# A two-layer scan kernel: sums over states taken once per turn, by halves, in shared PSUM banks

## The chip, the cores and the metric

The kernel runs on one core of a Trainium2 chip. The metric is the time of one execution on the device in microseconds (us). Engines are named as the profile does: PE (matrix), DVE (vector), ACT (activation), POOL (GpSimd), SP (issues the DMAs).

## The reference

A network of four layers works on images of shape (4, 96, 64, 64). Layer 0 is a convolution and selective scan with 192 channels and 16 states; layers 2 and 3 are spectral, attention and feed-forward blocks on tokens. The change concerns layer 1 alone, which applies this block (`ss2d`) twice in a row:

```
xz = x @ in_w.T;  xa, z = split(xz)
xc = silu(dwconv3x3(xa))                      # 96 channels, 4096 tokens
xs = 4 directions of xc: rows, columns, and both reversed
dts, Bs, Cs = split(xproj_w @ xs)             # 6, 8 and 8 rows
delta = softplus(dt_w @ dts + dt_b)
h[l] = exp(delta * A) * h[l-1] + delta * B[l] * xs[l]      # 8 states per channel
y[l] = sum over states of h[l] * C[l]  + D * xs[l]
out = (layernorm(sum of y over the 4 directions) * silu(z)) @ out_w.T
```

## The kernel before

Three stages follow each other: `stage_mamba` (layer 0), `stage_ss2d` (layer 1), `stage_tokens` (layers 2 and 3). The first two share the class `Scan`.

In layer 1 there are 8 blocks (4 images, 2 applications), 4 directions each, and 4 stretches of T = 1024 tokens per direction: 128 *turns*. A turn has 96 channels with 8 states, that is 768 rows, worked off as 6 *units* of 128 rows (16 channels by 8 states). So layer 1 has 768 units. For each unit:

- `load`: a DMA brings delta, each row spread over 8 partitions, into `sc_d` (6 buffers); for the third and the sixth unit of a turn another brings the inputs into `sc_u` (2 buffers).
- `decay`: ACT takes the exponential, in place in `sc_d`, or into PSUM for the third and sixth unit.
- `inputs`: for the other four units PE spreads the input over states, two matmuls of 512 columns into a tile `s` of two PSUM banks. There are 2 buffers of `s`; the third and sixth unit use one for the decay. `s` is free again once the unit's scan is done.
- `scan`: DVE multiplies `s` by B (rows in `bc`), then runs the scan over 1024 tokens, in place in `sc_d` (or `sc_u`). For the third and the sixth unit POOL does the multiplication by B in `sc_u`.
- `outputs`: POOL multiplies the states by C (the other half of `bc`) into a product `sc_h` (5 buffers, 4 KB per partition each).
- `reduce`: after every three units (a *round*) PE sums the products over states with a 0/1 table `c_red`: three matmuls side by side, into 32 rows each, for both halves of 512 tokens. The sums of both rounds accumulate in the tile `y`, [128, 1024] in two PSUM banks, one buffer.
- `end`: DVE adds `y` to `ysum`, 96x1024 at once; in the two directions by columns the access to `ysum` is strided.

In the profile a float32 matmul appears as two MATMUL rows. PSUM's eight banks before: two buffers of `s` (4 banks), one of `y` (2), two of `mm` (1 each). `mm` is shared by all other matmuls of layer 1: the projection to delta, B and C (`delta<-mm`), the row of C spread over partitions (`mm<-bc_stack,selbc`, copied to `bc` by ACT), a temporary of the splitting into bfloat16 parts (`bc_in`, `bc_part`), and the work between the scans of two blocks (convolution `mm<-xp,w_conv`, gates `ysum<-mm`, layer norm, output projection).

Nearly all instructions of layers 0 and 1 carry line 466, as they are recorded first (`Plan`) and issued by a helper. Their order on each engine is made beforehand: `Plan.order` simulates the five engines with a cost per operation and lets every engine take the ready operation with the lowest index, the index being the place in the program. A tile of `mm` is a *hold*: the simulation gives it one of the ring's buffers when the first operation is taken and frees it after the last; the first one waits for everything that later operations of the hold with lower-indexed inputs need. Buffers of other tags (`sc_h`, `s`, `y`, `bc_stack`) go round in fixed order. On the chip each engine then runs its list strictly in that order. DMAs are all issued from SP's queue.

The program order is given by `Scan.run`, step by step. In step s: loads of unit s+5; the paced work of the turn or block; `reduce` of the round that ends with unit s−3; `end` of the turn that ends with unit s−4; `scan` of unit s; decay and inputs of unit s+2; `outputs` of unit s.

The row of C of a turn passes through `narrow` (split into three bfloat16 parts, written to DRAM, read back as `bc_stack`, 2 buffers) and `mix` (two matmuls into `mm`, two copies to `bc`).

Of the kernel before, what the change touches and what calls it, by code (L numbers as in the profile page):

```python
# [11 lines left out]
F32 = mybir.dt.float32  # L12
BF16 = mybir.dt.bfloat16
# [4 lines left out]
PSUM = bass.MemoryType.PSUM  # L18
DRAM = bass.MemoryType.DRAM

NB, C, HW, L = 4, 96, 64, 4096
T, W = 1024, 512
NT, NW = L // T, L // W
DIN, NS0, RK = 192, 16, 6
NS1, NDIR = 8, 4
# [157 lines left out]
class Work:  # L183


    def __init__(self, steps, count, due):
        self.steps, self.count, self.due = steps, count, due
        self.taken, self.since, self.done = 0, None, False
# [92 lines left out]
class Plan:  # L281
# [174 lines left out]
    def run(self, tc):  # L456
        def placed(v, holds):
            hold = holds.get(v.tensor.name) if isinstance(v, bass.AP) else None
            return bass.AP(hold.buffer.tensor, v.offset, v.ap) if hold else v

        with tc.manual_schedule():
            for op in self.order():
                for method, a, kw in op.calls:
                    a = [placed(v, op.holds) for v in a]
                    kw = {n: placed(v, op.holds) for n, v in kw.items()}
                    getattr(getattr(self.nc, op.engine), method)(*a, **kw)  # L466
# [88 lines left out]
def split_steps(nc, x, parts, ps):  # L555


    p, n = x.shape
    for part in parts[0:2]:
        nc.scalar.copy(part, x)  # L560
        yield
        off = ps.tile([p, n], F32, tag="mm", name="off_ps")
        nc.scalar.copy(off, part)
        nc.vector.tensor_tensor(x, x, off, ALU.subtract)
        yield
    nc.scalar.copy(parts[2], x)
    yield
# [26 lines left out]
class Scan:  # L594
# [6 lines left out]

    LOOK = 5

    def __init__(self, k, rep, ps, n_state, red, bufs):
        self.k = k
        self.rep, self.ps, self.red, self.bufs = rep, ps, red, bufs
        self.ns, self.dl = n_state, 128 // n_state
        self.per = 32 // self.dl
        self.yps = None
# [37 lines left out]

    def decay(self, u):
        if not u.spread:
            u.s = self.ps.tile([128, T], F32, tag="s", name="s_ps", bufs=2)  # L650
            self.nc.scalar.activation(u.s, u.d, AF.Exp, scale=u.turn.acol(u.j))
        else:
            self.nc.scalar.activation(u.d, u.d, AF.Exp, scale=u.turn.acol(u.j))

    def inputs(self, u):
        u.s = self.ps.tile([128, T], F32, tag="s", name="s_ps", bufs=2)
        with self.nc.side_by_side(overlap=self.halves(u)):
            for h, (table, du) in enumerate(u.turn.spread(u)):
                self.nc.tensor.matmul(u.s[:, h * W:(h + 1) * W], table, du, start=True, stop=True)
# [24 lines left out]
    def reduce(self, us):  # L684
# [8 lines left out]
        for hs in halves:  # L693
            with nc.side_by_side():
                for h in hs:
                    for u in us:
# [3 lines left out]
                            start=not held, stop=r == self.per - 1, skip_group_check=True,  # L700
                        )

    def run(self, units, plan):


        nc = self.nc
        works = []
        for s in range(-self.LOOK, len(units) + 5):
            def at(n):
                return units[n] if 0 <= n < len(units) else None  # L710

            works += plan(s)
            u = at(s + self.LOOK)
            if u:
                if u.first:
                    u.turn.ready.finish()
                self.load(u)
            for w in works:
                w.pace(s)
            works = [w for w in works if not w.done]  # L720
            u = at(s - 3)
            if u and u is u.round[-1]:
                self.reduce(u.round)
            u = at(s - 4)
            if u and u.last:
                u.turn.end(u.q, self.yps)
            u = at(s + 2)
            if u and u.spread:
                self.decay(u)
            u = at(s)  # L730
            if u:
                self.scan(u)
            u = at(s + 2)
            if u:
                if not u.spread:
                    self.decay(u)
                else:
                    self.inputs(u)
            if u and not u.spread:
                nc.gpsimd.tensor_tensor(u.u, u.u, u.turn.bc[:, 0, :], ALU.mult)  # L740
            u = at(s)
            if u:
                self.outputs(u)
        for w in works:
            w.finish()
# [292 lines left out]
def stage_ss2d(ctx: ExitStack, k: Common, x: bass.AP, mid: bass.AP, bn: bass.AP, mid2: bass.AP):  # L1038
# [3 lines left out]
    nc, tc = k.nc, k.tc  # L1042
    wp = ctx.enter_context(tc.tile_pool(name="s_w", bufs=1))
    big = ctx.enter_context(tc.tile_pool(name="s_big", bufs=1))
    pl = Plan(nc)
    big = pl.pool(big, 2)
    wk = pl.pool(ctx.enter_context(tc.tile_pool(name="s_wk", bufs=1)), 2)
    rep = pl.pool(ctx.enter_context(tc.tile_pool(name="s_rep", bufs=1)), 4)
    dr = pl.pool(ctx.enter_context(tc.tile_pool(name="s_dr", bufs=1, space=DRAM)), 3)
    ps = pl.pool(ctx.enter_context(tc.tile_pool(name="s_ps", bufs=1, space=PSUM)), 2, {"mm": [128, W]})  # L1050
    NCH = C // 16
    PW = HW + 2

# [3 lines left out]
    out_w = k.load(wp, "w_out1")  # L1057
    group = k.load(wp, "c_group")
    sel = k.load(wp, "c_sel1")
    sc = Scan(k, rep, ps, NS1, k.load(wp, "c_red1"), (6, 2, 5))  # L1060
    nc.scalar.activation(acol, acol, AF.Exp)
    nc.vector.tensor_scalar(acol, acol, -1.0, None, ALU.mult)
    selbc = wp.tile([3 * NS1, 128], BF16, name="selbc")
# [33 lines left out]
    nc = k.nc = pl  # L1097
# [4 lines left out]
    class Block:  # L1102


        def __init__(self, b, i):
            self.b, self.i, self.rows = b, i, 0
            self.ready = None
# [111 lines left out]
    class Tokens(Turn):  # L1219
# [56 lines left out]
        def narrow(self):  # L1276

            x = wk.tile([64, 128], F32, tag="bc_in", name="bc_in", bufs=1)
            part = [(128, 8), (T, NS1), (1, 128)]
            at = self.dd[C + NS1:CD, :]  # L1280
            nc.sync.dma_start(out=x, in_=bass.AP(at.tensor, at.offset, part))
            yield
            parts = [wk.tile([64, 128], BF16, tag="bc_part%d" % n, name="bc_part", bufs=1) for n in range(3)]
            yield from split_steps(nc, x, parts, ps)
            sd = dr.tile([3, NS1, T], BF16, tag="bcd", name="bcd", bufs=3)
            for n, p in enumerate(parts):
                nc.sync.dma_start(out=bass.AP(sd.tensor, sd[n].offset, part), in_=p)
            self.stack = wk.tile([3 * NS1, T], BF16, tag="bc_stack", name="bc_stack", bufs=2)
            nc.sync.dma_start(out=self.stack, in_=sd.rearrange("n r t -> (n r) t"))

        def mix(self):
# [10 lines left out]
                nc.scalar.copy(self.bc[:, 1, at:at + W], pb)  # L1302
                yield

        def end(self, q, yps):
            ysum, t, yps = self.block.ysum, self.t, yps[0:C, :]
            cs = slice(t * T, (t + 1) * T)
            if self.d == 0:
                nc.vector.scalar_tensor_tensor(
                    ysum[:, cs], self.block.xc[:, cs], dsum[:, self.block.i:self.block.i + 1], yps,  # L1310
                    ALU.mult, ALU.add,
                )
            elif self.d % 2 == 0:
                nc.vector.tensor_tensor(ysum[:, cs], ysum[:, cs], yps, ALU.add)
            else:
                n_w = T // HW
                view = ysum.rearrange("p (h w) -> p w h", w=HW)[:, n_w * t:n_w * (t + 1), :]
                nc.vector.tensor_tensor(view, view, yps.rearrange("p (w h) -> p w h", h=HW), ALU.add)

    blocks = [Block(b, i) for pair in ((0, 1), (2, 3)) for i in range(2) for b in pair]  # L1320
# [6 lines left out]
    units = [u for turn in turns for u in sc.units(turn, (groups,))]  # L1327
# [326 lines left out]
@with_exitstack  # L1654
def kernel(ctx: ExitStack, tc: tile.TileContext, x: bass.AP, w: dict, out: bass.AP):
    k = Common(ctx, tc, w)
    dp = ctx.enter_context(tc.tile_pool(name="mids", bufs=1, space=DRAM))
    mid = dp.tile([NB, C, L], F32, name="mid")
    mid2 = dp.tile([NB, C, L], F32, name="mid2")
    bn = k.cp.tile([C, 2], F32, name="bn_scale")  # L1660
    stage_mamba(k, x, mid, bn)
    stage_ss2d(k, x, mid, bn, mid2)
    stage_tokens(k, mid2, out)
# [22 lines left out]
```

## Time and profile before

| | |
|---|---|
| median of three runs | 7542.12 us (7540.26 to 7549.51) |
| profiled execution | 7571.38 us, span 7569.0 us |
| layer 0, layer 1, layers 2 and 3 in the span | 0 to 2890, 2890 to 6235, 6235 to 7569 us |
| busy over the span | PE 6648.2, DVE 5764.4, POOL 5765.3, ACT 4499.9 us |
| mean granted PE clock | 0.905 |

The profile is one execution. In its page the span is cut into 40 slices, with a digit for the busy tenths of each engine. A group row has the operation, out<-in by tile names, shapes, count, busy us and mean ns, then the engine's idle time before it and who ended it. A wait row has who waited for whom, the total in us, the times and the longest. A timeline row has start, duration, engine and operation, and in brackets the idle time before it and its releaser. A window row has the stretch, its length, the busy us of PE, PE's weight loads, DVE, ACT and POOL, the granted clock, the busy share of the DMA engines and GB/s.

### The profile page before, as it was taken

The numbers are of one execution on the slowest core, as the hardware profiler recorded it, in microseconds if no ns is written. First come the engines' busy times: TensorE is split into PE (matmuls) and PEld (weight loads), VectorE is DVE, ScalarE is ACT, GpSimd is POOL, SyncE is SP. The second block draws the span as 40 slices with busy tenths as digits, with TensorE's granted clock in tenths as the row PEclk, the third lists the DMA queues.
The fourth block names the chain that finished last, engine by engine and source line by source line (L and its number), as shares of the span: only waits on it lengthen the run. The fifth ranks groups of instructions, "written<-read, shape, count | busy, mean of one in ns | idle before, by whom it ended". The sixth has DMA issues, their size and how long they took to land. (4 is left out here: it accounts for less than half of the span.)

```text
span 7569.0 us, 84054 instructions
## 1 busy us (share of the span) xinstructions
PE 6648.2 (88%) x28616; PEld 2867.8 (38%) x28616; DVE 5764.4 (76%) x4491; ACT 4499.9 (59%) x6656; POOL 5765.3 (76%) x2836
## 2 busy tenths in 40 slices
PE   8888888988888877989898898989898868999997
PEld 3322233323323222323232333323232228778784
DVE  6989988988898985898887878788888863344342
ACT  4655555555555544777777676677777644445442
POOL 6989988989998985889897978889898870232323
PEclk9999999999999998999898898989898888889897
DMA  7988988988888886999898989899999960000000
GB/s 192 239 224 232 230 216 220 239 222 226 227 235 217 222 224 168 233 241 230 223 234 222 244 218 241 215 230 232 230 238 238 236 176 22 1 18 5 15 9 9
DMA packets 448078, 1418.13 MB, mean 187 GB/s; under 512 B 81626, under 2 KB 91539, under 8 KB 445600
## 3 DMA queue, kind: packets, MB, share of 16 engines
q1 hardware_dynamic: 447648, 1412.76, 72.7%
q8 instruction: 225, 3.69, 0.2%
q14 instruction: 205, 1.68, 0.1%
HBM read 1238.48 MB, written 174.06 MB: 187 GB/s over the span
## 5 line engine op out<-in xcount | busy, mean ns | idle before, releaser
L466 POOL TENSOR_TENSOR sc_h<-sc_d,bc 128x1024 f32<-128x1024 f32 x1024 | 2406.9, 2360 | 394.8 <-DVE sc_d L466 186.0
L466 DVE TENSOR_TENSOR_SCAN sc_d<-sc_d,carry,s 128x1024 f32<-128x1024 f32 x768 | 1799.7, 2344 | 74.7 <-ACT sc_d L466 18.2
L466 DVE TENSOR_TENSOR s<-s,bc 128x1024 f32<-128x1024 f32 x1024 | 1248.7, 1220 | 505.3 <-PE s L466 500.2
L466 PE MATMUL s<-du,c_sel 96*128 96x512 f32 x2048 | 1124.0, 678 | 226.6 <-DVE sc_d L466 127.3
L466 ACT ACTIVATE sc_d<-sc_d,w_alog 128x1024 f32<-128x1024 f32 x1024 | 1165.7, 1144 | 257.4 <-DMA sc_d<-dd 253.7
L466 POOL TENSOR_TENSOR sc_h<-sc_u,bc 128x1024 f32<-128x1024 f32 x512 | 1208.0, 2359 | 112.2 <-PE y L466 73.1
L466 POOL TENSOR_TENSOR sc_u<-sc_u,bc 128x1024 f32<-128x1024 f32 x512 | 1208.2, 2360 | 100.9 <-DMA sc_u<-ud 87.6
L466 PE MATMUL y<-sc_h,c_red 128*32 128x512 f32 x6144 | 1094.5, 656 | 87.2 <-POOL sc_h L466 83.2
L466 DVE TENSOR_TENSOR_SCAN sc_u<-s,carry,sc_u 128x1024 f32<-128x1024 f32 x384 | 895.2, 2331 | 36.7 <-ACT s L466 17.5
L466 PE MATMUL s<-du,c_selp 128*128 128x512 f32 x1408 | 729.8, 647 | 112.3 <-DVE sc_d L466 108.8
L466 PEld LDWEIGHTS s<-du,c_sel 96*128 96x128 f32 x2048 | 396.2, 208 | 869.8 <-issue 427.7
L466 ACT ACTIVATE s<-sc_d,w_alog 128x1024 f32<-128x1024 f32 x512 | 570.8, 1115 | 240.7 <-DVE sc_d L466 155.7
L466 ACT ACT_TABLE_LOAD x499 | 640.2, 1283 | 8.7
L466 DVE TENSOR_TENSOR_SCAN sc_d<-sc_d,s 128x1024 f32<-128x1024 f32 x256 | 583.1, 2282 | 23.0 <-ACT sc_d L466 6.2
L508 POOL TENSOR_TENSOR ln_rs<-ln_rs_e,mhalf 128x4 f32<-128x4 f32 x128 | 134.9, 1056 | 582.9 <-DVE ln_rs_e L506 581.2
L466 PE MATMUL mm<-xp,w_conv 96*96 96x512 f32 x1152 | 528.7, 600 | 4.6 <-ACT bc L466 2.2
L466 PEld LDWEIGHTS y<-sc_h,c_red 128*32 128x32 f32 x6144 | 197.7, 114 | 848.9 <-issue 529.7
L466 ACT COPY carry<-sc_d 128x1 f32<-128x1 f32 x768 | 142.8, 186 | 565.5 <-DVE sc_d L466 564.0
L466 PEld LDWEIGHTS s<-du,c_selp 128*128 128x128 f32 x1408 | 263.2, 201 | 539.4 <-issue 274.7
L466 PE MATMUL mm<-hn,conv_w 97*64 97x512 f32 (+1 forms) x1024 | 368.8, 615 | 22.5 <-DVE hn L466 22.5
L466 PEld LDWEIGHTS mm<-xp,w_conv 96*96 96x96 f32 x1152 | 185.3, 164 | 310.1 <-issue 295.5
L466 DVE TENSOR_TENSOR_SCAN sc_u<-s,sc_u 128x1024 f32<-128x1024 f32 x128 | 290.7, 2271 | 14.1 <-ACT s L466 7.9
(211 smaller groups left out, 9343.6 us busy)
## 6 DMA issues: line engine op xcount, KB each, us to landing
sc_d<-dd SPq DMA_DIRECT2D x1536, 512.0 KB
sc_u<-ud SPq DMA_DIRECT2D x512, 512.0 KB
bc<-dd SPq DMA_DIRECT2D x128, 512.0 KB
dd<-delta SPq DMA_DIRECT2D x128, 448.0 KB
bc<-bcd SPq DMA_DIRECT2D x64, 512.0 KB
ud<-du SPq DMA_DIRECT2D x192, 128.0 KB
dd<-delta SPq DMA_DIRECT2D x32, 512.0 KB
ud<-du SPq DMA_DIRECT2D x32, 512.0 KB
```

The source lines that it names most:

```text
L466: getattr(getattr(self.nc, op.engine), method)(*a, **kw)
L508: nc.gpsimd.tensor_tensor(rs, ve, self.mhalf[:p, 0:n], ALU.pow)
```

## The change

In layer 1 the sums are no longer taken round by round. All six products of a turn are kept, and in the step of unit s = last + 2 a new method `sums` takes them all: for each half of 512 tokens it opens a tile of `mm` (one bank), accumulates the two rounds in it, and calls `end` for that half, which adds 96x512 to `ysum`. The tile `y` is not used in layer 1 any more; its two banks go to `mm`, which has 4 buffers. `sc_h` gets 8 buffers instead of 5, `bc_stack` 1 instead of 2. `s` keeps its 2 buffers. Layer 0 uses the same class with the old behaviour.

```diff
-    def __init__(self, k, rep, ps, n_state, red, bufs):
+    def __init__(self, k, rep, ps, n_state, red, bufs, spreads=2, late=False):
...
+    def sums(self, us):
+
+        nc = self.nc
+        for h in range(T // W):
+            yps = self.ps.tile([128, W], F32, tag="mm", name="y_ps")
+            for r in range(self.per):
+                with nc.side_by_side():
+                    for u in us:
+                        if u.r == r:
+                            row, _, at = u.rows[h]
+                            nc.tensor.matmul(
+                                yps[row:row + 32, :], self.red[:, r, :], u.c[:, at:at + W],
+                                start=r == 0, stop=r == self.per - 1, skip_group_check=True,
+                            )
+            us[0].turn.end(h, yps)
...
+            u = at(s - 2)
+            if self.late and u and u.last:
+                self.sums(units[s - 1 - len(u.round) * self.per:s - 1])
             u = at(s - 3)
-            if u and u is u.round[-1]:
+            if not self.late and u and u is u.round[-1]:
                 self.reduce(u.round)
             u = at(s - 4)
-            if u and u.last:
+            if not self.late and u and u.last:
                 u.turn.end(u.q, self.yps)
...
-    ps = pl.pool(ctx.enter_context(tc.tile_pool(name="s_ps", bufs=1, space=PSUM)), 2, {"mm": [128, W]})
+    ps = pl.pool(ctx.enter_context(tc.tile_pool(name="s_ps", bufs=1, space=PSUM)), 4, {"mm": [128, W]})
...
-    sc = Scan(k, rep, ps, NS1, k.load(wp, "c_red1"), (6, 2, 5))
+    sc = Scan(k, rep, ps, NS1, k.load(wp, "c_red1"), (6, 2, 8), 2, True)
...
-            self.stack = wk.tile([3 * NS1, T], BF16, tag="bc_stack", name="bc_stack", bufs=2)
+            self.stack = wk.tile([3 * NS1, T], BF16, tag="bc_stack", name="bc_stack", bufs=1)
...
-        def end(self, q, yps):
-            ysum, t, yps = self.block.ysum, self.t, yps[0:C, :]
-            cs = slice(t * T, (t + 1) * T)
+        def end(self, h, yps):
+            ysum, yps, at = self.block.ysum, yps[0:C, :], self.t * T + h * W
+            cs = slice(at, at + W)
...
-                n_w = T // HW
-                view = ysum.rearrange("p (h w) -> p w h", w=HW)[:, n_w * t:n_w * (t + 1), :]
+                view = ysum.rearrange("p (h w) -> p w h", w=HW)[:, at // HW:(at + W) // HW, :]
```

More of the change, by code (lines that the diff above doesn't have):

```diff
@@ L602 @@
     LOOK = 5
-    def __init__(self, k, rep, ps, n_state, red, bufs):
-        self.k = k
+    def __init__(self, k, rep, ps, n_state, red, bufs, spreads=2, late=False):
+        self.k, self.spreads, self.late = k, spreads, late
         self.rep, self.ps, self.red, self.bufs = rep, ps, red, bufs
@@ L649, in decay @@
         if not u.spread:
-            u.s = self.ps.tile([128, T], F32, tag="s", name="s_ps", bufs=2)
+            u.s = self.ps.tile([128, T], F32, tag="s", name="s_ps", bufs=self.spreads)
             self.nc.scalar.activation(u.s, u.d, AF.Exp, scale=u.turn.acol(u.j))
@@ L655, in inputs @@
     def inputs(self, u):
-        u.s = self.ps.tile([128, T], F32, tag="s", name="s_ps", bufs=2)
+        u.s = self.ps.tile([128, T], F32, tag="s", name="s_ps", bufs=self.spreads)
         with self.nc.side_by_side(overlap=self.halves(u)):
```

## The prediction

> **What bounds the kernel now.** I read the page's slices first, then the busy time by stretch, then the waits inside the stretch that the change touches, then the groups there, and last one turn in the timeline.
>
> ```profile
> span 7569.0 us, 84054 instructions
> ...
> PE   8888888988888877989898898989898868999997
> ...
> DVE  6989988988898985898887878788888863344342
> ...
> POOL 6989988989998985889897978889898870232323
> PEclk9999999999999998999898898989898888889897
> ```
>
> PE, DVE and POOL are all busy for eight to nine tenths until slice 32, and no slice shows one of them alone at its limit. The change touches only layer 1. Its scan runs from about 2890 us to 6235 us.
>
> ```profile
> core 0: us, PE busy (x) PEld busy (x) DVE busy (x) ACT busy (x) POOL busy (x), PEclk, DMA share, GB/s
> 0.00:2890.00 2890.00, 2520.65 (x8660) 853.49 (x8660) 2534.01 (x1606) 1597.27 (x2170) 2546.34 (x1124) 0.93 0.86 222
> 3020.00:6180.00 3160.00, 2758.23 (x8098) 943.33 (x8097) 2681.46 (x1815) 2226.11 (x3326) 2794.27 (x1271) 0.91 0.91 230
> 5400.00:5800.00 400.00, 363.86 (x1086) 124.37 (x1087) 349.29 (x235) 290.81 (x439) 369.58 (x168) 0.92 0.94 237
> ```
>
> The second row is the full-speed part of layer 1: 128 turns in 3160 us, 24.7 us each. Per turn PE is busy 21.5 us, DVE 20.9, POOL 21.8; each idles 3 to 4 us. The three hand work to each other through small buffers, so a time lost on one is partly lost on all. The third row is the fastest stretch: DMA moves 237 GB/s where the mean is 230.
>
> ```profile
> DVE s L466 <- PE s L466: 266.4, 165, 5.0
> ...
> PE s L466 <- DVE sc_d L466: 127.3, 75, 7.2
> ...
> POOL sc_h L466 <- ACT bc L466: 90.1, 26, 9.5
> ...
> POOL sc_h L466 <- PE y L466: 82.2, 32, 6.6
> ...
> PE mm L466 <- ACT bc L466: 28.8, 39, 4.0
> ```
>
> These are waits in 3020:6180 (total us, times, longest). The largest is DVE's on `s`: two buffers of `s` go round between PE and DVE. PE can refill one only after a scan frees it, and DVE needs it one unit later. The `mm` waits are PE waiting for a shared bank to be emptied.
>
> ```profile
> 4998.59 3.78 PE L466 MATMUL s<-du,c_sel 96*128 96x512 f32 x4 [2.87 <-DVE sc_d L466]
> ...
> 5002.30 1.03 PE L466 MATMUL mm<-bc_stack,selbc 24*128 24x512 bf16 x2
> ...
> 5004.09 4.66 POOL L466 TENSOR_TENSOR sc_h<-sc_d,bc 128x1024 f32<-128x1024 f32 x2 [9.46 <-ACT bc L466]
> ```
>
> Here POOL stands 9.46 us for a row of C (`bc`) whose matmul ran late among the shared banks. PE, after 2.87 us of idleness, took 3.78 us for a fill of `s` that takes 1.98 us elsewhere (at 4319.04).
>
> **The change, part by part.** I weigh each effect over 128 turns. Because three engines take turns at being the bound, a removed wait on one counts by about 0.4 (my choice, between a third and a half).
>
> *Matmuls of the sums.* They are 24 per turn before and after (3,072 in all), in groups of three side by side. PE work: 0. What changes is when they run. Before, a round of three products is summed by 12 matmuls in about 2.3 us (rows of 1.92, 2.29 and 2.69 us in the timeline), twice per turn at different steps. After, all 24 become ready at once with the turn's sixth product, about 4.6 us, and they come in program order ahead of the fill of `s` of the same step. A fill takes 2.2 us (1112.5 us for 506). DVE covers it with a multiply and a scan, 1.22 + 2.34 = 3.56 us. Before, a fill that meets a round is late by at most 2.3 + 2.2 − 3.56 = 0.94 us, twice a turn; after, by at most 4.6 + 2.2 − 3.56 = 3.24 us, once. Taking half of each as the mean: 0.94 against 1.62 us per turn, so **+86 us**. Bounds: 0, if all falls into PE's 3.1 us of idleness per turn, and 3.24 × 128 = +415 us, if each meets in full.
>
> *PE's wait.* All sums now wait for one product. Behind them on PE stand the next fills and DVE waits for those. The present wait of matmul `y` on POOL is 25.6 us in 27 times; I leave it, between 0 and twice that.
>
> *The clock.* The half of the turn that loses a round has more idleness: 1.6 + 2.3 = 3.9 us, in pieces. The row at 4998.59 shows that 2.87 us of idleness went with a fill 1.8 us longer. The Trainium skill ("TensorE: Matmul & The Clock Gate", section on HAM oscillation) allows gaps up to about 3.4 us. By the rule these pieces cost 0. By the row, if one turn in five gets such a gap, 26 × 1.8 = 46 us of PE time, 0.4 of it on the path. I follow the row: **+20 us**, bounds −58 (clock from 0.91 to 0.95, half on the path) to +58.
>
> *Evacuations on DVE.* One 96x1024 read becomes two of 96x512. Contiguous: 2 × 0.67 (`ysum<-ysum,mm` has 669 ns) for 1.24 us; strided: 2 × 1.27 (`t<-t,o`, 1269 ns) for 2.40 us. That is 0.10 × 64 + 0.14 × 64 = 15 us, and 8 us on the path. Behind each on DVE stand multiply and scan; the second eviction can wait for the second half of the sums. The present wait is 33.1 us in 24 times; up to once more of it, taken at +7. Together **+15 us**.
>
> *Products kept.* POOL makes the same six per turn (2.36 us each). Before, five buffers: the third and the sixth product of a turn wait for a round's release. After, eight buffers: only the third product of the next turn waits, again with two products in between, but for the third of four groups instead of the second of two, 1.15 us later. From 82.2 us in 32 times (2.6 us each) I make 16 times 3.75 = 60 us: −22 × 0.4 = **−9 us**, bounds −82 and +150.
>
> *Four shared banks.* This is the gain. PE waits for banks: 28.8 (`bc`) + 17.7 (`ysum`) + 16.4 (`delta`) + 14.0 (`bc_in`) + 10.2 (DVE `ysum`) = 87.1 us; POOL's wait on `bc` is 90.1 us. Together 177.2 us, the most these rows can give back; the least is 0, as the sums now take two of the banks for a few us per turn and some of these waits are for data. The same page of the skill, same section, reports that doubling PSUM buffers gave no further gain in its kernel. By the rule 0, by the rows 0.4 × 177 = 70. I take the rows, for they name the bank's reader: **−70 us**.
>
> *One `bc_stack` instead of two.* Its load on SP's queue now also waits for the last `bc` matmul of the turn before; queued behind it are `sc_d` and `sc_u` loads. In the late turn shown, the stack was issued at 4988.14 and read at 5002.30; the next is due a turn (24.7 us) after, so some 10 us of margin remain even there. Cost 0; without that margin POOL's waits on `sc_u` (31.9 us) could double: +30. No DMA is added or moved otherwise.
>
> Sum: 86 + 20 + 15 − 9 − 70 = **+42 us**. The profiled execution took 7571.4 us (span 7569.0 and 2.4 around), 29 us over the median of 7542.1; against itself the sum gives 7613, against the median 7584.
>
> **The rivals.**
>
> *B, the banks win.* The order of instructions is made by a list scheduler; with four banks it can fill PE's gaps (402 us idle in 3160) with shared matmuls, so fewer fills are late. For it: two of three engines' waits name banks; the latest `bc` turns idle POOL for 9 us. Against it: the largest wait, 266 us on `s`, keeps its two buffers. Price: 0.6 × 177 = −106, the burst at a third, +30: 7466 us. It cannot go far: the fastest stretch moves 237 against 230 GB/s, 3% of 3160, or some 95 us.
>
> *C, the products come free too late.* One mechanism: POOL makes two products and one or two multiplies after the last product, 7.1 to 9.4 us, and then needs the third group of sums done. In the turn shown the last product of a round ended at 4992.3 and its round at 4995.7, 3.4 us; one more group makes 4.6, inside 7.1. It decides from the point where PE's queue delays the sums by over 2.5 us. At 1.2 us per turn POOL gives away 154 us: 7696 us. For it: the 6.6 us maximum of that wait; against: the wait has half as many places.
>
> *D, no change.* The scheduler spreads the groups between fills, and bank relief and delays cancel: 7542 us.
>
> **How the numbers follow.** A (the sum, 7584; its own range 7558 to 7650) has 0.40; B 0.36; C 0.15; D 0.09. A and B differ in two sizes only, the burst's and the banks'; I put A ahead because the burst is bounded by 0 and +415, far wider above my value than below, while the banks cannot give more than 177. About 0.2% (15 us) is what a measurement can tell: faster 0.36, same 0.10 (D and the edge of A), slower 0.54. The range reaches from 7430 (B with nearly all of the relief) to 7725 (C with A's evictions).
>
> **What would show it.** Right: in layer 1 DVE's wait on `s` rises from 266 us by 50 to 150; POOL's wait on `bc` falls below 60; PE's waits on ACT for `mm` fall below half; the sums appear as runs of about 24 matmuls; `ysum` evictions at 0.67 and 1.27 us; PEclk at or below 0.91. Wrong: DVE's wait on `s` falls and the 3160 us stretch shortens (B), or POOL's wait on the sums passes 150 us (C). 0 to 2890 us must stay as it is; if it moves, the whole reading is off.

## The result: no change, and the profile after

The changed kernel takes 7540.5 us (median of 12 runs), the kernel before 7546.8 us (12 runs). The ratio is 0.9993, with a 95% interval from 0.9982 to 1.0004: no difference that can be measured. I had forecast 7584 us, +0.5%; the time lies inside the range, but no rise came. What came true is rival D, to which I had given 0.09. Below, each ratio is to the kernel before, run beside the kernel in question, and ratios are turned into microseconds on 7546.8 us.

The page of the profile after, the same rows as were shown of before:

```profile
span 7542.1 us, 84090 instructions
...
PE   8888889988888887989797798989898769999997
...
DVE  6989988988898985888888888888898863344342
...
POOL 6989988989898985889897879889898960232323
PEclk9999999999999998989898898989897878889897
```

No digit differs from before by more than one. The stretches and the waits of layer 1 tell more. First the stretches (length, busy us of PE, weight loads, DVE, ACT, POOL, then granted clock, DMA share, GB/s):

```profile
0.00:2890.00 2890.00, 2512.39 (x8660) 852.60 (x8660) 2537.01 (x1617) 1597.61 (x2171) 2548.31 (x1126) 0.94 0.85 222
...
3020.00:6180.00 3160.00, 2729.15 (x8153) 980.89 (x8151) 2684.59 (x1942) 2230.46 (x3339) 2792.34 (x1273) 0.88 0.91 230
```

Layer 0 is as it was. In layer 1 the engines do in 3160 us almost exactly what they did before (POOL 2792.3 against 2794.3 us, DVE 2684.6 against 2681.5), but PE runs at a granted clock of 0.88 instead of 0.91. The waits of the changed kernel in 3020:6180 (total us, times, longest):

```profile
DVE s L466 <- PE s L466: 261.6, 178, 4.2
PE s L466 <- DVE sc_d L466: 260.3, 101, 7.1
...
DVE ysum L466 <- PE mm L466: 77.8, 65, 4.5
POOL sc_h L466 <- ACT bc L466: 68.7, 21, 8.8
...
POOL sc_h L466 <- PE mm L466: 40.4, 25, 3.4
...
PE mm L466 <- DMA bc_stack<-bcd: 30.8, 18, 6.6
...
PE mm L466 <- ACT bc L466: 6.8, 9, 1.7
```

The four banks did what they were to do. The five waits of PE on a bank's reader that made 87.1 us before are now 6.8 (`bc`) + 3.3 (`ysum`) + 1.2 (`delta`) + 4.4 (`bc_in`) + 2.6 (DVE `ysum`) = 18.3 us; POOL's wait on `bc` fell from 90.1 to 68.7 us and its wait on the sums from 82.2 to 40.4 us. But PE's wait for a scan to free a buffer of `s` doubled, from 127.3 to 260.3 us. What the banks gave, PE stands about again, elsewhere. Its idle time in the stretch is about what it was (402 us before, 431 after), but in the timeline the pieces longer than 2 us have grown from 48 (150 us together) to 78 (291 us).

The timeline also shows the late sums themselves (start, duration, then engine, operation and count of rows; the fills are two together):

```profile
3170.48 3.63 PE L466 MATMUL mm<-sc_h,c_red 128*32 128x512 f32 x24
3174.05 3.81 PE L466 MATMUL s<-du,c_sel 96*128 96x512 f32 x8
```

In about half of the turns all 24 rows of a turn's sums stand in one run like this; in most of the others they come as two runs of 12, with other matmuls between.

So the change has either two effects of opposite sign, or only effects that nothing depends on. The experiments were made to tell these apart.

### The profile page after: what moved, and what is told of

It is laid out like the page before. It is cut to its first block, busy times and chain, and to the rows that moved or that the text cites. A ratio compares the mean times of both kernels' runs of the same rounds, so it can differ in the third digit from the quotient of the medians.

```text
span 7542.1 us, 84090 instructions
## 1 busy us (share of the span) xinstructions
PE 6589.2 (87%) x28616; PEld 2890.5 (38%) x28616; DVE 5771.9 (77%) x4619; ACT 4498.6 (60%) x6664; POOL 5765.3 (76%) x2836
## 5 line engine op out<-in xcount | busy, mean ns | idle before, releaser
L466 PE MATMUL s<-du,c_sel 96*128 96x512 f32 x2048 | 1180.1, 711 | 313.9 <-DVE sc_d L466 260.3
L466 PEld LDWEIGHTS s<-du,c_sel 96*128 96x128 f32 x2048 | 420.7, 220 | 985.3 <-issue 434.5
L466 DVE TENSOR_TENSOR_SCAN sc_d<-sc_d,s 128x1024 f32<-128x1024 f32 x256 | 582.9, 2282 | 29.5 <-ACT sc_d L466 13.4
L466 PE MATMUL mm<-sc_h,c_red 128*32 128x512 f32 x3072 | 533.4, 638 | 14.7 <-POOL sc_h L466 11.6
L466 PE MATMUL y<-sc_h,c_red 128*32 128x512 f32 x3072 | 489.5, 658 | 58.0 <-POOL sc_h L466 57.6
L466 POOL TENSOR_TENSOR du<-delta,xc 96x1024 f32<-96x1024 f32 (+2 forms) x128 | 266.8, 2089 | 91.4 <-ACT delta L466 48.7
L466 DVE TENSOR_TENSOR ysum<-ysum,mm 96x512 f32<-96x512 f32 x256 | 248.1, 972 | 80.2 <-PE mm L466 78.9
```

## The experiments

**First batch: the two halves of the change.** Theory T1: the four banks gain, the late sums lose, and the two cancel. Theory T2: the exchange of `s` holds layer 1, and it is indifferent to both.

*e1_late_mm2*, the change with two shared banks:

```diff
-    ps = pl.pool(... name="s_ps" ..., 4, {"mm": [128, W]})
+    ps = pl.pool(... name="s_ps" ..., 2, {"mm": [128, W]})
```

> The change with two shared banks instead of four, so only the sums at the turn's end, the eight products and the halves are left. Theory T1 (the four banks gain and the late sums lose, and the two cancel): slower than before by 50 to 120 us, as the loss stands alone, with PE's waits on shared banks above the 87 us of before. Theory T2 (layer 1 is held by the exchange of the two buffers of s between PE and DVE, to which both parts are indifferent): within 20 us of before, with DVE's wait on s at 250 to 280 us in 3020:6180.

Measured: 7790.8 us, ratio 1.0331 (1.0309 to 1.0352), +250 us. T2 is out: the late sums without the two banks lose more than twice what T1 said at most. The waits of this kernel show the loss in all three engines, DVE on `s`, POOL on the sums, PE on banks:

```profile
DVE s L466 <- PE s L466: 341.9, 191, 7.0
...
POOL sc_h L466 <- PE mm L466: 105.6, 41, 7.3
...
PE mm L466 <- ACT bc L466: 36.8, 49, 2.5
```

*e2_late_s3*, the freed banks given to a third `s` instead:

```diff
-    ps = pl.pool(... name="s_ps" ..., 4, {"mm": [128, W]})
+    ps = pl.pool(... name="s_ps" ..., 2, {"mm": [128, W]})
-    sc = Scan(k, rep, ps, NS1, k.load(wp, "c_red1"), (6, 2, 8), 2, True)
+    sc = Scan(k, rep, ps, NS1, k.load(wp, "c_red1"), (6, 2, 8), 3, True)
```

> The change with the two banks that were freed given to a third buffer of s, and two shared banks. T2: DVE's wait on s (262 us after the change) falls below 130 us, and the time falls by 60 to 150 us. T1: a third s does little (within 30 us of the kernel with two shared banks and two s), as the banks and the burst decide.

Measured: 7652.8 us, ratio 1.0142 (1.0120 to 1.0164). Against e1 a third `s` is worth 143 us, so `s` does matter, as T2 said; but the same two banks used as shared ones are worth 255 us. DVE's wait on `s` fell from 341.9 to 191.3 us, not below 130.

*e3_sums_behind_fill*, the sums moved in the step:

```diff
-            u = at(s - 2)
-            if self.late and u and u.last:
-                self.sums(...)
             u = at(s - 3)
...
             if u and not u.spread:
                 nc.gpsimd.tensor_tensor(u.u, u.u, u.turn.bc[:, 0, :], ALU.mult)
+            u = at(s - 2)
+            if self.late and u and u.last:
+                self.sums(...)
```

> The change, with the sums placed behind the fill of s of the same step in program order instead of ahead of it. T1 (the burst ahead of the fill costs): faster than the change by 30 to 90 us, DVE's wait on s below 200 us. T2: within 20 us of the change.

Measured: 7535.3 us, ratio 0.9992 (0.9981 to 1.0003), the same as the change. That the sums stand ahead of the fill in program order costs nothing that can be measured. My picture of the burst, a block of sums in front of a fill of the same step, is not shown to be how the late sums lose.

*e4_before_keep8*, the kernel before with the buffers of the change:

```diff
-    sc = Scan(k, rep, ps, NS1, k.load(wp, "c_red1"), (6, 2, 5))
+    sc = Scan(k, rep, ps, NS1, k.load(wp, "c_red1"), (6, 2, 8))
-            self.stack = wk.tile(... name="bc_stack", bufs=2)
+            self.stack = wk.tile(... name="bc_stack", bufs=1)
```

> The kernel before with eight buffers of sc_h instead of five and one of bc_stack instead of two, nothing else. Both theories: POOL's wait on the sums (82 us in 3020:6180) goes to near zero. T1: worth 0.4 of it, 20 to 40 us. T2: within 15 us of before.

Measured: 7524.3 us, ratio 0.9975 (0.9959 to 0.9990), −19 us. POOL's wait on `y`, 82.2 us before, is no longer among its waits; so a wait of 82 us, wholly removed, was worth some 19 us. One `bc_stack` costs nothing that shows here.

**Second batch: sharing, or lateness?** Theory S: e1 loses because the sums sit in the banks that the others need. Theory L: because the sums are late and in one piece.

*e5_late_own2_mm2* and *e6_late_own1_mm3*, the late sums in banks of their own:

```diff
-            yps = self.ps.tile([128, W], F32, tag="mm", name="y_ps")
+            yps = self.ps.tile([128, W], F32, tag="y", name="y_ps", bufs=2)   # e6: bufs=1
-    ps = pl.pool(... name="s_ps" ..., 4, {"mm": [128, W]})
+    ps = pl.pool(... name="s_ps" ..., 2, {"mm": [128, W]})                    # e6: 3
```

> The late sums by halves in two banks of their own and two shared banks for the rest: the PSUM of before, with only the moment of the sums, the halves and the products changed. Theory S (the 251 us lost with two shared banks come from the sums sitting in the banks that the other matmuls need): within 25 us of before, 7520 to 7565 us, PE's granted clock in layer 1 back at 0.90 or more. Theory L (they come from the sums being late and in one piece): 7680 us or more, clock below 0.87.

> The late sums in one bank of their own and three shared banks for the rest. S: 7480 to 7540 us, as the others now have three banks for themselves, and the second half waits a little for the first half's eviction. L: 7600 us or more, as the sums come as late and as one piece as in the change.

*e7_late_mm3*, the change with three shared banks, sums included (the 4 of the pool line made a 3):

> The change with three shared banks, sums included. S: between the change (7540) and two banks (7791), nearer to the change: 7560 to 7640 us. L: within 30 us of either end, as banks are not what loses.

Measured: e5 7540.7 us, ratio 0.9984 (0.9974 to 0.9995); e6 7564.8 us, 1.0013 (1.0001 to 1.0025), slower than S had it; e7 7624.1 us, 1.0079 (1.0048 to 1.0110). The shared banks make a clear series, sums included: two +250, three +60, four −5 us. At first sight S alone explains e1. But e5 has a flaw: a tile with a fixed ring is not a hold for the planner, so in e5 and e6 the first round of sums may start as soon as its three products are made. Their sums are late in program order only.

**Third batch: the flaw mended, and what holds layer 1.**

*e8_late_own2_one_piece*, as e5, with the two own banks as holds:

```diff
-    ps = pl.pool(... name="s_ps" ..., 4, {"mm": [128, W]})
+    ps = pl.pool(... name="s_ps" ..., 2, {"mm": [128, W], "y": [128, W]})
```

> As the late sums in two banks of their own, but the two banks are handled by the planner as the shared ones are, so that no sum of a turn starts before its sixth product is made: late and in one piece, without sharing. Theory S (sharing is what lost 251 us with two banks): within 25 us of the kernel with own banks, 7515 to 7565 us. Theory L (late and in one piece): 7650 us or more. If both have a part, between.

Measured: 7662.4 us, ratio 1.0166 (1.0149 to 1.0184), +125 us. With nothing shared, waiting for the sixth product costs 137 us against e5. (As holds, the two banks are also given out by the planner and no longer in fixed order, so this step is not quite lateness alone; e13 below lifts only the wait.) So both theories hold for one half: from e5 to e8 137 us for lateness (L), from e8 to e1 125 us for sharing two banks (S); and from e8 to the change −130 us for making one pool of four out of two and two. The stretch of e5, then that of e8:

```profile
3020.00:6180.00 3160.00, 2749.62 (x8093) 951.61 (x8091) 2699.32 (x1939) 2234.76 (x3330) 2788.84 (x1268) 0.90 0.91 230
```

```profile
3020.00:6180.00 3160.00, 2744.38 (x7891) 977.40 (x7890) 2611.43 (x1884) 2183.68 (x3256) 2705.80 (x1233) 0.86 0.88 224
```

And the waits, of e5 and of e8:

```profile
DVE s L466 <- PE s L466: 236.3, 157, 6.3
...
DVE ysum L466 <- PE y L466: 51.0, 47, 4.5
```

```profile
DVE s L466 <- PE s L466: 294.0, 206, 4.2
...
DVE ysum L466 <- PE y L466: 79.0, 64, 4.5
...
POOL sc_h L466 <- PE y L466: 39.9, 17, 3.5
```

PE is as busy as in e5 while DVE and POOL get less done, at a clock of 0.86. On DVE, which is busy 88 us less, the loss shows as waits on PE: 58 us more on `s` and 28 us more on the sums. POOL's wait on the sums is half that of the kernel before: it is not the kept products that lose.

*e9_after_half_fill* and *e11_before_half_fill* leave out the second of the two matmuls of each fill from the third turn on, in the change and in the kernel before, so that half of the scan's input is what stood in the buffer; *e10_after_conv2* takes PE work away elsewhere, seven of the nine taps of the change's convolution:

```diff
-            for h, (table, du) in enumerate(u.turn.spread(u)):
+            for h, (table, du) in enumerate(u.turn.spread(u)[0:1 if self.ns == NS1 and u.turn.n > 1 else 2]):
```

```diff
-                for tap in range(9):
+                for tap in range(2):                    # e10, in convolve
...
-                        start=tap == 0, stop=tap == 8,
+                        start=tap == 0, stop=tap == 1,
```

> The change with the second of the two matmuls of each fill of s left out from the third turn on (that half of the scan's input is what stood in the buffer); PE does 2.2 us less... half of each fill, some 4.4 us per turn. Theory X (what holds layer 1 now is the exchange of the two buffers of s): DVE's wait on s falls below 120 us, and the time by 100 to 300 us. Theory Y (DVE, POOL and DMA hold it anyway): less than 60 us.

> The change with the convolution of layer 1 cut from nine taps to two: PE has some 3 us less to do per turn, but not in the exchange of s. X: DVE's wait on s falls little (200 us or more stay) and the time by less than 60 us. Theory P (PE's load as such holds layer 1): the time falls nearly as much as with the half fill, 100 us or more.

> The kernel before with the same second matmul of each fill of s left out. X: the same fall as in the change, within 40 us of its time, as s holds both. If the four shared banks help once s is no longer the limit, the change with the half fill is faster than this by over 40 us.

Measured: e9 7448.3 us, ratio 0.9880 (0.9864 to 0.9895), −91 us, with DVE's wait on `s` at 162.5 us; e10 7555.7 us, 1.0016 (1.0005 to 1.0026), with that wait risen to 317.1 us; e11 7542.4 us, 0.9997 (0.9987 to 1.0006). The stretch of e10:

```profile
3020.00:6180.00 3160.00, 2488.25 (x7271) 875.40 (x7266) 2660.19 (x1928) 2172.03 (x3283) 2774.94 (x1265) 0.83 0.90 228
```

PE's busy time is 241 us less than in the change (2488.3 against 2729.2), and no time is gained. So PE's total of work does not hold layer 1. That is not as clean as it looks, though, as the fills got slower at the same time (713 to 757 ns a row, at a clock of 0.83). A shorter fill makes the change 85 us faster, between what theories X and Y asked, and does not help the kernel before at all, against theory X. So the two kernels, equal in time, are not held by the same thing: after the change a shorter exchange of `s` pays, before it does not. Which part of the change makes that difference no run shows.

**Last batch: the clock, and lateness in the pool of four.**

*e12_after_warm* adds two matmuls per turn where PE idles now:

```diff
+        if self.late and u.index == 3:
+            t = self.ps.tile([128, W], F32, tag="mm", name="warm")
+            for h in range(2):
+                nc.tensor.matmul(
+                    t[0:32, :], self.red[:, 0, :], u.h[:, h * W:(h + 1) * W], start=True, stop=True
+                )
```

> The change with two extra matmuls per turn whose result nobody reads (a shared bank, 512 columns each, fed by the fourth unit's scan), laid into the stretch in which PE now idles, before the first fill of the next turn. Theory K (part of the loss of the late sums is PE's clock, which falls in that idle stretch): the granted clock in 3020:6180 rises from 0.88 to 0.90 or more, the four matmul rows of a fill shorten from 711 to below 690 ns on the mean, and the time falls by 15 to 60 us although PE does more. Theory N (the clock does not matter, the work does): the time rises by 10 us or more, whatever the clock does.

Measured: 7541.3 us, ratio 0.9997 (0.9985 to 1.0009), no change. The fill (mean ns of a row after the busy us, then PE's idle time before it) in 3020:6180 of the kernel before, of the change, and of e12:

```profile
L466 PE MATMUL s<-du,c_sel 96*128 96x512 f32 x2024 | 1112.5, 679 | 226.6 <-DVE sc_d L466 127.3 <-DVE sc_u L466 72.5 <-DVE ln_rs_e L466 15.9
```

```profile
L466 PE MATMUL s<-du,c_sel 96*128 96x512 f32 x2016 | 1165.3, 713 | 313.9 <-DVE sc_d L466 260.3 <-DVE sc_u L466 49.4 <-DVE ln_rs_e L466 3.0
```

```profile
L466 PE MATMUL s<-du,c_sel 96*128 96x512 f32 x2016 | 1036.3, 642 | 167.1 <-DVE sc_d L466 103.4 <-DVE sc_u L466 56.3 <-ACT sc_d L466 5.0
...
L466 PE MATMUL mm<-sc_d,c_red 128*32 128x512 f32 x504 | 256.6, 634 | 75.5 <-DVE sc_d L466 66.5 <-ACT bc L466 5.2 <-DVE bc_in L466 1.2
```

The clock did all that theory K wanted: 0.95 granted in this stretch, fills from 713 to 642 ns a row, DVE's wait on `s` from 261.6 to 176.7 us. The time stayed. Other waits grew: POOL's on the sums from 40.4 to 76.2 us, and ACT's on the loads of `sc_d` from 99.2 to 160.4 us. Neither K nor N is borne out. That the 257 us of added matmuls ate the gain of the clock is likely but not shown, and so is whether a higher clock without them would gain.

*e13_after_early_sums* lets the banks of the sums open once the first round's products are there:

```diff
+            if not hold.early:
                 first.after |= {by for op in hold.ops for by in op.after if by.index < first.index}
...
             yps = self.ps.tile([128, W], F32, tag="mm", name="y_ps")
+            nc.holds[yps.tensor.name].early = True
```

> The change, with the banks of the sums opened as soon as the first three products are made (the first round of sums no longer waits for the sixth product), still in the four shared banks. Theory S+L (late sums cost about 120 us and the pool of four gives as much back because late sums hold their banks only briefly): no gain, within 30 us of the change, as the two sums hold two of the four banks for half of the turn. If the lateness alone costs and the banks' time does not matter: faster than the change by 60 us or more.

Measured: 7497.2 us, ratio 0.9936 (0.9921 to 0.9951), −48 us. This version beats both kernels. Against the change, not waiting for the sixth product is worth 43 us: more than S+L allowed, less than the other theory asked. With e5 and e8 this makes a table of two by two (time against the kernel before, all with halves and eight products):

| | sums may start with the third product | sums wait for the sixth |
|---|---|---|
| two own banks, two shared | e5: −12 us | e8: +125 us |
| one pool of four | e13: −48 us | the change: −5 us |

The pool of four is worth 130 us where the sums are late and 36 us where they are not. Most of what it gives to the change is the mending of what lateness broke. (In e5 the own banks go round in fixed order, in the other three the planner gives them out.)

The stretch of e13 and its waits on `s`:

```profile
3020.00:6180.00 3160.00, 2752.82 (x8224) 958.17 (x8220) 2707.92 (x1975) 2243.50 (x3347) 2802.33 (x1285) 0.91 0.91 231
```

```profile
DVE s L468 <- PE s L468: 220.4, 139, 3.8
...
PE s L468 <- DVE sc_d L468: 119.1, 76, 5.4
```

PE's wait for a scan in `sc_d` is back at 119 us (before: 127) and the clock at 0.91, without any added work. Its wait for one in `sc_u` is longer, 109.5 us (before: 72.5). POOL and DVE get a little more done in the same time than in either kernel.

## Why the prediction was wrong, point by point

- **Matmuls of the sums (+86), with the clock (+20), the evacuations (+15) and the kept products (−9): +112.** The total of the late sums was about right, in part by luck. e8 is just this part of the change, late and in one piece by halves with eight products, in the PSUM of before: +125 us. The mechanism was only half right. e3 shows that in the change the place ahead of the fill costs nothing that can be measured; what costs is that no sum may start before the sixth product (e5 against e8, +137). I had that wait in the text and left it as it was. The run of sums is also shorter than I took it: 24 rows, that is 12 float32 matmuls and not 24, in 3.63 us, where I had 4.6.
- **The clock:** it fell from 0.91 to 0.88, and a row of the fill went from 679 to 713 ns, 69 us over 2016 rows, where I had 46 us of PE time. The idle time did not stay in small pieces. Fills after idle pieces of about the same length came out unlike each other (in the kernel before 1.98 us after 2.41 us, at 3357.71, and 3.78 us after 2.16 us, at 4950.30), so neither the rule nor my one row prices a piece. What the clock is worth in time stays open: e12 raised it without any gain.
- **Four shared banks (−70): this step failed.** The direction was right: PE's waits on the banks' readers fell from 87.1 to 18.3 us. But the term was mis-sized. In the change, where the sums are late, it measured −130 us (e8 to the change); where they are not, −36 us (e5 to e13). I had priced it from the wait rows of the kernel before, times a factor of 0.4 of my own choice, and those rows cannot hold the delays that the late sums bring and the four banks then take away. With −130 in place of −70 the sum would have been −18 us, close to the measured −5. Why four banks relieve late sums by so much is not settled: from e8 to the change the waits that I had counted fall only from 172.4 to 87.0 us. That the planner, with more banks, also finds a better order is likely but not shown. The report that doubling PSUM buffers gave no further gain (the Trainium skill, "TensorE: Matmul & The Clock Gate", section on HAM oscillation) does not carry over to this kernel: with the late sums in the pool, the time falls by 190 us from two to three shared banks and by 65 from three to four.
- **The parts do not simply add.** Lateness costs 137 us with two banks for the sums and two for the rest, and 43 us in a pool of four. A sum of separately priced terms cannot show that.
- **Products kept (−9) and one `bc_stack` (0):** e4 gives −19 us for both; the wait of POOL on the sums halved in the change, as said (82.2 to 40.4 us; I had 60). Rival C is refuted by it. In the change PE's matmuls waited longer for the load of `bc_stack` than before (13.4 us, now 30.8), which I had put at nothing.
- **Evacuations (+15):** the halves came near the price. In 3020:6180 the group `ysum<-ysum,mm` has 252 reads in 245.4 us; taking 124 of them (60 of layer norm, 64 of the one row direction in this group) at 0.67 us leaves 1.27 us for each of the 128 strided ones, as I had it. DVE's waits on PE before it adds to `ysum` rose from 33.1 (sums) + 14.1 (layer norm) to 77.8 us for both, +31, at the top of my bound of one more such wait.
- **What I had named as signs:** PEclk at or below 0.91 (0.88), PE's waits on ACT for banks below half (yes), evictions at the lengths given (yes), layer 0 untouched (yes), runs of 24 rows of sums (in about half of the turns), POOL's wait on `bc` below 60 us (no, 68.7). DVE's wait on `s` was to rise by 50 to 150 us and did not (266.4 to 261.6): that row already said that the slow side had been compensated.
- **Rival B** came nearer to what the banks gave the change (−106) but took the burst at a third; **D** named the outcome and half of the cause, relief and delays cancelling, at a chance far too low. Its other half, the sums spread between fills, holds for some of the turns only. A sum of opposite terms of 112 and 70, whose largest parts were each bounded by 0 below, should have left more room for zero.

## What to carry to other kernels

When a change gives a resource with one hand and takes it with the other, run each half alone, and then in all combinations: two kernels of equal time here hide +125 and −130 us, and the second figure is −36 when the first is taken away. Wait rows of the kernel before cannot price a relief from waits that the change itself brings. And where a buffer pool is shared, look at when a holder may open and must close: letting the sums open their banks early turned a change of no effect into a gain of 0.64%.

## What was not expected of the hardware

With matmuls taken away so that PE was busy 241 us less (e10), PE's granted clock fell from 0.88 to 0.83 and a row of the fill grew from 713 to 757 ns. With 257 us of matmuls added (e12) the clock rose to 0.95, a row shortened to 642 ns, and PE was busy only 91 us more in all (2820.2 against 2729.2). Neither moved the time by more than 0.3%. In this stage a PE with less to do was also a slower PE.
